# A six-layer decoder on one core: keys leave a PSUM bank by one engine, a second norm takes its variance from the first, and the planner lets layer 1's keys and values fill gaps only

## Chip, core and metric

The kernel runs on one core of a Trainium2 chip. The metric is the device time of one execution in microseconds; each kernel is run several times and the median counts. One more execution was recorded by the hardware profiler. All times below are in microseconds unless marked ns.

The core has five engines that matter here: PE (TensorE, matmuls and transposes into PSUM; PEld is its weight load), DVE (VectorE), ACT (ScalarE), POOL (GpSimd) and SP (SyncE, which issues all DMAs of this kernel). PSUM is used as eight banks of 128 partitions x 512 floats.

## What is computed

A decoder of two post-norm layers on x of shape (8, 256, 256), that is eight sequences (b = 0 to 7) of 256 tokens with 256 features. Each sub-layer is added to its input and normed:

```python
x = ln(x + gated_linear_recurrence(x))                      # l0a
x = ln(x + xattn(x, ctx, ctx, mask, bias))                  # l0x: 16 heads of 16
x = ln(x + ffn0(x))                                         # l0f, below
x = ln(x + self_attn(x, rel_k, rel_v))                      # l1a: relative positions, clipped at 20
x = ln(x + xattn(x, ctx, ctx, mask1))                       # l1x
x = ln(x + swiglu(x))                                       # l1f: hidden 768
# ffn0: a norm of its own, then a quantisation with ONE scale for the whole batch
xn = (x - mu) * rsqrt(var + 1e-5) * gamma + beta
scale = max(abs(xn)) / 127;  xq = round(clip(xn / scale)) * scale
out = xq @ ternary(weight).T
```

`ln` subtracts the mean and divides by sqrt(var + 1e-5), without gain or bias. The one scale of ffn0 is a barrier: no sequence can enter l0f before the last one has left l0x.

## The kernel before, in words

**Tiling.** Per sequence, x is held with tokens on partitions (two tiles of 128 tokens) and, transposed by PE, as xT with features on partitions (two chunks of 128). An attention item (class Item) is one attention of one sequence; ai is 0 for layer 0's cross-attention, 1 for layer 1's self-attention, 2 for layer 1's cross-attention. It has 16 heads, worked in four quads (n = 0 to 3) of four heads.

**One item.** project_q and project_k (line 784) multiply xT or ctxT with weights (PROJ, eight matmuls, one bank) and copy the result out of the bank. Keys are written twice, each time multiplied by par, a column of ones and zeros per partition, so that the heads of even and odd number do not mix (m = 0, 1). For self-attention there are two kinds of keys (k and kr: two different constants are added for far positions). Each piece of keys (chunk c, parity m) was an own step for which the planner picked DVE (line 800) or ACT (line 804). quad (line 845) then issues the scores (line 859) into four banks, at most one quad of an item after another; per head, DVE adds a bias, mask or band and takes the row minimum (line 890, tile sn), ACT takes the exponential (line 906, tile p), PE transposes it (line 470, tile pt), ACT or DVE copies that to SBUF (tile pts, lines 261 and 262), and values (line 929) multiplies it with v (line 944, tile pv). attend_out (line 964) divides by the sums, projects (pso), adds (line 1010) and norms.

**Norms.** norm (line 495) takes bn_stats and bn_aggr on DVE (lines 503, 505), 1/sqrt(var + eps) on POOL as an add and a power (lines 508, 509) and scales on DVE (line 514). own_norm (line 1027) norms l0x once more (tiles st_f0n, rs_f0n, xn), transposes it (ps_xn), applies gamma and beta (xnT, line 1038) and takes the largest absolute value (line 1054, events "amax"). barrier (line 1112) waits for all eight, reduces them over partitions (ps_amax line 1125, gmax, ps_gmax line 1136) and makes the scale; quantised (line 1153) then runs ffn0 per sequence (xq line 1169, psf, yf line 1178, norm l0f, ps_l0f).

**Self-attention's bands.** to_scratch (line 1242) multiplies q with the relative keys (psr line 1252), widens the result on POOL (w, ends; lines 1263, 1266) and writes it to DRAM (sk, line 1272), per chunk c. to_bands (line 1282) fills a band tile on POOL (line 1290) and reads it back skewed, with four DMAs (line 1302), per quad; it sets the event ("band", n). In item_s1 (line 1231) the order was: project_q, to_scratch(0) and to_bands(0), project_k, to_scratch(1) and to_bands(1), a slot of acc, then the first quad. In quad, the scores were issued first and only DVE's step waited for the band.

**Layer 1's cross-attention.** keys_values (line 1468) computes its keys and values from the context alone, once per sequence (psk of ctxT, copied by lines 1479 or 1482; psv of ctxT, copied by line 1503), and stores them in DRAM; it starts once the last item of layer 0 has its q. item_x1 (line 1512) loads them (kin line 1521, vin line 1523), and multiplies the keys with par on DVE (line 1540) or POOL (line 1541).

**The order of work.** Nothing is ordered by loops. Every step is a generator's request to Order.run (line 128): engine, planned cost in us, time at which its inputs are ready. The planner keeps a clock for each engine, and always emits the request with the earliest planned start, in steps of 0.1; ties go by urgency (a smaller number is more urgent: items by 100 + 40 x position, keys_values by 5000 + b). A step that may run on either of two engines takes the one that ends first. Emission fixes each engine's program order, and each engine works through its list in that order. Buffers are slots: p 3, pts 8, q 3, k 2, ctx 2, PSUM banks 8, acc 2; a request for slots waits until they are dropped, the most urgent first. Costs are planned, so a wrong cost changes the order but not what a step takes.

Of the kernel before, what the change touches and what calls it, by code (L numbers as in the profile page):

```python
# [8 lines left out]
F32 = mybir.dt.float32  # L9
# [65 lines left out]

class Order:
# [51 lines left out]
    def run(self):  # L128
        while self.tasks:
            self.serve()  # L130
            best = None
            for task in self.tasks:
# [3 lines left out]
                for engine, cost, emit in ways:  # L136
                    start = max(self.free[engine], ready)
                    if engine == "PE" and kind != self.kind:
                        start += self.TURN[self.kind + kind]
                    late = 0.0 if len(ways) == 1 else start + cost  # L140
                    key = (round(start * 10), task[0], late, task[1])
                    if best is None or key < best[0]:
                        best = (key, task, engine, cost, emit, start, kind)
# [49 lines left out]
def kernel(  # L193
# [80 lines left out]
    half = const.tile([P, NQ], F32, name="half")  # L274
# [220 lines left out]
    def norm(y, t_y, make, name):  # L495

        st = small.tile([P, NQ, 6], F32, tag="ln_st", name=f"st_{name}")
        mv = small.tile([P, NQ, 2], F32, tag="ln_mv", name=f"mv_{name}")
        rstd = small.tile([P, NQ], F32, tag="ln_rs", name=f"rs_{name}")
# [7 lines left out]
        def root():  # L507
            nc.gpsimd.tensor_scalar(rstd, mv[:, :, 1], 1.0, EPS, ALU.mult, ALU.add)
            nc.gpsimd.tensor_tensor(rstd, rstd, half, ALU.pow)

        def scaled():
            dst = make()
            for t in range(NQ):
                nc.vector.tensor_scalar(
                    dst[:, t, :], y[:, t, :], mv[:, t, 0:1], rstd[:, t : t + 1], ALU.subtract,
# [4 lines left out]
        t = yield from do("POOL", 0.95, [t], root)  # L520
        return (yield from do("DVE", 0.68, [t], scaled))
# [98 lines left out]
    def recurrence(b):  # L620
# [9 lines left out]
        def emit():  # L630
# [9 lines left out]
            "POOL", 0.7, [t, a.at],  # L640
# [77 lines left out]
    NS = 2 * KC  # L718

# [35 lines left out]
    def project_q(it, srcT, t_src):  # L755
# [16 lines left out]
        def dve():  # L772
# [6 lines left out]
            [t, t_b, it.q.at], ("ACT", 2 * on_act(256), act), ("DVE", 2 * on_dve(256), dve)  # L779
# [4 lines left out]
    def project_k(it, srcT, t_src, kinds):  # L784
# [9 lines left out]
        it.k, it.t_k = [], []  # L794
        for bufs, bias, biasp, lo, hi in kinds:
            k = yield from get(bufs, f"k{it.name}_{len(it.k)}", t_ps)
            it.k.append(k)
            for c in range(KC):
                for m in range(2):
                    dve = lambda: nc.vector.tensor_scalar(  # L800
                        k.tile[:, c, m, :], ps.tile[:, c, lo:hi], bias(c), par[:, m : m + 1], ALU.add,
                        ALU.mult,
                    )
                    act = lambda: nc.scalar.activation(  # L804
                        k.tile[:, c, m, :], ps.tile[:, c, lo:hi], AF.Identity, bias=biasp(c, m),
                        scale=par[:, m : m + 1],
                    )
                    t = yield from either(
                        [t_ps, t_b, k.at],
                        ("DVE", on_dve(hi - lo) + 0.12, dve), ("ACT", on_act(hi - lo) + 0.09, act),  # L810
                    )
                    it.t_k.append(t)
# [32 lines left out]
    def quad(it, n, parts, bias):  # L845


        c, i = divmod(n, 2)
        if n == 0 and it.ai != 1:
            it.sums = small.tile([P, NQ, H], F32, tag="sums", name=f"sums{it.name}")  # L850
        at = max([it.t_q, *it.t_k])
# [27 lines left out]
        t_bias = 0.0  # L879
        if it.ai == 1:  # L880
            t_bias = yield from event(it.key("band", n))
# [82 lines left out]
    def attend_out(it, t_pv):  # L964
# [47 lines left out]
        ps.drop(t)  # L1012
        t = yield from settle(xb.tile, t, b, it.result, xb.drop)
        events["xs " + it.result, b] = t
        if ai == 0:
            yield from own_norm(b, t)
        elif ai == 1:
# [9 lines left out]
    def own_norm(b, t):  # L1027

        xn = yield from get(y_bufs, f"xn{b}", t)
        t = yield from norm(xs[b], max(t, xn.at), lambda: xn.tile, f"f0n{b}")  # L1030
# [19 lines left out]
        t = yield from either([t], ("DVE", 2 * on_dve(256), dve), ("ACT", 2 * on_act(256), act))  # L1050
# [180 lines left out]
    def item_s1(b, kr_bufs, wide_bufs, acc_bufs, tail_bufs, at_bufs, band_bufs):  # L1231
# [10 lines left out]
        def to_scratch(c, t_sk):  # L1242
# [4 lines left out]
            for t in range(NQ):  # L1247
# [20 lines left out]
                t_w = yield from do("POOL", 0.85, [t_w], emit)  # L1268
# [13 lines left out]
        def to_bands(c, times, sk_set):  # L1282
            for i in range(2):
# [11 lines left out]
                t_f = yield from do("POOL", 0.75, [band.at, it.t_ends[c]], emit)  # L1295
# [26 lines left out]
        def tails_task(n, p, left, t_p):  # L1322
# [33 lines left out]
            t = yield from do("POOL", 1.3, [t_p, tail.at], emit)  # L1356
# [85 lines left out]
        times = yield from to_scratch(1, t_rel)  # L1442
        order.spawn(urgency(it, 0, -19), to_bands(1, times, sk_set))
# [6 lines left out]
        )  # L1450
        events["fed", 1, b] = it.t_q
# [16 lines left out]
    def keys_values(b):  # L1468
# [8 lines left out]
        t_k = []  # L1477
        for c in range(KC):
            dve = lambda: nc.vector.tensor_scalar(
                k.tile[:, c, :], ps.tile[:, c, :], qkb[:, 5, c : c + 1], None, ALU.add  # L1480
            )
            act = lambda: nc.scalar.activation(
                k.tile[:, c, :], ps.tile[:, c, :], AF.Identity, bias=qkb[:, 5, c : c + 1], scale=1.0
            )
            t_k.append(
                (
                    yield from either(
                        [t, t_b, k.at], ("DVE", on_dve(256) + 0.12, dve), ("ACT", on_act(256) + 0.09, act)
                    )
                )  # L1490
            )
        ps.drop(max(t_k))
        t_k = yield from dma(t_k, 262144, lambda: nc.sync.dma_start(out=xk[b], in_=k.tile))
# [18 lines left out]
    def item_x1(b):  # L1512
# [23 lines left out]
        for m in range(2):  # L1536
            dst = k.tile[:, :, m, :]
            t = yield from either(
                [t_k, k.at],
# [252 lines left out]
```

## Time and profile before

| | us |
|---|---|
| three runs | 856.34, 852.46, 856.68 |
| median | 856.34 |
| the profiled execution | 851.82 |
| its span, first to last instruction | 850.1 |
| PE busy | 801.4 (94%) |
| DVE busy | 711.8 (84%) |
| ACT busy | 638.3 (75%) |
| POOL busy | 238.2 (28%) |

How the profile is read: the busy time of an engine is the time in which it has an instruction; matmuls are pipelined, so PE is drawn busy until the modelled end of one. In a timeline a line gives start, length, engine, source line, operation, output tile and inputs, how many instructions are merged (x8), and in brackets how long the engine was idle before and what ended that. In a table by stretches the columns are the busy time of each engine with its instruction count, and then the clock granted to PE (1.00 is full speed). The chain of waits is followed back from the last instruction. Names of tiles leave buffer numbers out: psk<-ctxT,wqk is a projection of keys from the context, psk<-xT_l0f one of layer 1's self-attention.

### The profile page before, as it was taken

How to read it: one execution, taken by the hardware profiler on the slowest of the kernel's cores; microseconds unless marked ns; L12 is line 12 of the kernel's file. 1: busy time of each engine (PE TensorE's matmuls, PEld its weight loads, DVE VectorE, ACT ScalarE, POOL GpSimd, SP SyncE). 2: the span in 40 equal slices, each digit the busy share in tenths (PEclk: the TensorE clock that was granted, in tenths of full speed). 3: DMA queues.
4: the chain of work that ended last, by engine and by line, in shares of the span. 5: the costliest groups of instructions: out<-in, count | busy, mean ns of one | idle time of the engine just before them, and what ended most of it. 6: DMA issues, size and time to landing. Idle time of an engine off the chain costs nothing.

```text
span 850.1 us, 21190 instructions
## 1 busy us (share of the span) xinstructions
PE 801.4 (94%) x7175; PEld 616.7 (73%) x7175; DVE 711.8 (84%) x2495; ACT 638.3 (75%) x2047; POOL 238.2 (28%) x419
## 2 busy tenths in 40 slices
PE   7998999999999988899899999999999998999985
PEld 6785766877777766567667777776777766888885
DVE  3979989998897797788779889898798987889785
ACT  2338987999996445798889898998899895948631
POOL 3440301221121043236144242342152334110020
PEclk9999999999999997999999999999999998999998
DMA  5729511101102446789755546656283432100000
GB/s 174 249 76 105 50 38 39 38 5 35 39 15 75 162 101 150 150 159 194 156 114 111 110 102 134 119 109 141 67 172 67 93 87 76 38 20 7 26 27 25
DMA packets 177681, 77.67 MB, mean 91 GB/s; under 512 B 155046, under 2 KB 171430, under 8 KB 177574
## 3 DMA queue, kind: packets, MB, share of 16 engines
q1 hardware_dynamic: 177574, 76.32, 40.6%
q8 instruction: 57, 0.93, 0.5%
q14 instruction: 50, 0.41, 0.2%
HBM read 41.66 MB, written 34.64 MB: 90 GB/s over the span
## 4 chain that ended last, share of the span: by engine, by line
PE 57%; ACT 15%; DVE 15%; issue 6%; DMA 3%; POOL 3%; SPq 2%; POOLq 0%; DVEq 0%; ACTq 0%
PE pt L470 13%; ACT p L906 9%; PE s L859 8%; PE pv L944 7%; PE psv L487 5%; DVE sn L890 4%; PE psk L476 4%; PE pso L487 4%; PE psq L476 3%; ACT pts L262 3%; PE psd L1667 2%; PE psr L1252 1%; DVE k L800 1%; ACT k L804 1%; SPq L389 1%
## 5 line engine op out<-in xcount | busy, mean ns | idle before, releaser
L906 ACT ACTIVATE p<-sn,nm 128x256 f32<-128x256 f32 x768 | 381.0, 506 | 27.9 <-DVE nm L890 25.6
L470 PE MATMUL pt<-ident,p 128*128 128x128 f32 x1536 | 213.6, 279 | 8.7 <-ACT p L906 2.8
L470 PEld LDWEIGHTS pt<-ident,p 128*128 128x128 f32 x1536 | 172.9, 142 | 52.4 <-ACT p L906 25.1
L262 ACT COPY pts<-pt 128x512 f32<-128x512 f32 x277 | 149.2, 586 | 39.3 <-PE pt L470 34.4
L906 ACT ACTIVATION_READ_ACCUMULATOR p<-sn,nm 128x1 f32 x768 | 151.6, 197 | 0.0
L859 PE MATMUL s<-k,q 32*128 32x256 f32 (+2 forms) x1792 | 134.0, 375 | 3.2 <-DVE nm L890 2.4
L859 PEld LDWEIGHTS s<-k,q 32*128 32x128 f32 x1792 | 87.5, 186 | 34.4 <-issue 14.0
L890 DVE CUSTOM_DVE_ANT_0 sn<-s,hide 128x256 f32<-128x256 f32 x256 | 93.7, 417 | 15.4 <-PE s L859 8.7
L944 PE MATMUL pv<-pts,v 128*32 128x256 f32 x1536 | 104.8, 384 | 0.7 <-ACT pts L262 0.7
L890 DVE CUSTOM_DVE_ANT_0 sn<-s,band 128x256 f32<-128x256 f32 x256 | 93.6, 416 | 12.9 <-ACT p L906 7.7
L890 DVE CUSTOM_DVE_ANT_0 sn<-s,bias 128x256 f32<-128x256 f32 x256 | 94.4, 419 | 10.1 <-ACT p L906 7.5
L261 DVE COPY pts<-pt 128x512 f32<-128x512 f32 x107 | 71.7, 683 | 4.3 <-PE pt L470 3.6
L944 PEld LDWEIGHTS pv<-pts,v 128*32 128x32 f32 x1536 | 43.1, 109 | 41.3 <-issue 17.9
L890 DVE DVE_READ_ACCUMULATOR2_ANT nm<- 128x1 f32 x768 | 62.9, 82 | 0.0
L975 POOL COPY rsw<-rsum 128x512 f32<-128x512 f32 x24 | 14.7, 612 | 130.3 <-DVE rsum L969 122.8
L487 PE MATMUL pso<-wvo,oT 128*128 128x256 f32 x192 | 47.9, 394 | 0.2 <-DVE oT L990 0.2
L487 PEld LDWEIGHTS pso<-wvo,oT 128*128 128x128 f32 x192 | 36.2, 196 | 6.7 <-DVE oT L990 1.4
L1290 POOL COPY band<-ends 64x256 f32<-64x256 f32 x64 | 22.3, 372 | 44.8 <-DVE nm L890 44.8
L1263 POOL COPY w<-w 128x504 f32<-128x504 f32 x32 | 19.6, 613 | 53.3 <-DVE w L261 31.4
L1362 DVE TENSOR_REDUCE acc<-tail 128x8 f32<-128x864 f32 x32 | 33.3, 1042 | 0.6 <-POOL tail L1351 0.6
L487 PE MATMUL psv<-wvo,ctxT 128*128 128x256 f32 x128 | 31.0, 385 | 0.1
L476 PE MATMUL psk<-ctxT,wqk 128*128 128x256 f32 x128 | 30.9, 384 | 0.0
(201 smaller groups left out, 1364.8 us busy)
## 6 DMA issues: line engine op xcount, KB each, us to landing
sk<-w SPq DMA_DIRECT2D x32, 416.0 KB
band<-sk SPq DMA_DIRECT2D x64, 104.0 KB
pb<-p SPq DMA_DIRECT2D x64, 104.0 KB
band<-sk SPq DMA_DIRECT2D x64, 84.0 KB
pb<-p SPq DMA_DIRECT2D x64, 84.0 KB
acc<-pb SPq DMA_DIRECT2D x32, 156.0 KB
ctxT<-in_ctxT SPq DMA_DIRECT2D x16, 256.0 KB
wpad<-in_qk_w SPq DMA_DIRECT2D x6, 512.0 KB
```

What stands on the lines that cost most here:

```text
L261: ("DVE", on_dve(n), lambda: nc.vector.tensor_copy(dst, src)),
L262: ("ACT", on_act(n), lambda: nc.scalar.copy(dst, src)),
L470: nc.tensor.transpose(ps[:, c, t * P : (t + 1) * P], src[:, t, c * P : (c + 1) * P], ident)
L476: nc.tensor.matmul(ps, w[:, c, lo:hi], rhs[:, c, :], start=(c == 0), stop=(c == KC - 1))
L487: nc.tensor.matmul(ps[:, t, :], srcT[:, c, t * P : (t + 1) * P], w[:, c, :], start=(c == 0), stop=(c == KC - 1),)
L859: nc.tensor.matmul(ps[j].tile[:, t, first : first + w], it.q.tile[32 * j : 32 * j + 32, c, t * P : (t + 1) * P], k[32 * j : 32 * j + 32, c ...
L890: nc.vector.tensor_tensor_reduce(out=s.tile[:, t, :], in0=ps[j].tile[:, t, :], in1=tile[:, t, :], scale=-1.0, scalar=3e38, op0=ALU.add, op ...
L906: nc.scalar.activation(p.tile[:, j, q, :], s.tile[:, q, :], AF.Exp, bias=nm[:, q : q + 1], scale=-1.0, accum_out=it.sum_of(q, h),)
L944: nc.tensor.matmul(it.pv.tile[32 * j : 32 * j + 32, c, :], it.v.tile[:, k, head_of(n, j), :], pts.tile[:, k, :], start=(k == 0 and i == 0 ...
L1263: nc.gpsimd.tensor_copy(w.tile[:, :, NR:], w.tile[:, :, NR - 1 : NR].to_broadcast([P, HH, PBW - NR]))
L1290: nc.gpsimd.tensor_copy(band.tile[0:BLK, :, t, lo:hi], it.ends[c][0:BLK, t, i:HH:2].unsqueeze(2).to_broadcast([BLK, 4, hi - lo]),)
L1362: lambda: nc.vector.tensor_reduce(acc[:, c, :, own, 1], tail.tile, AX.X, ALU.add),
```

## The change

- **The planner** (Order.run): a step of keys_values (urgency at or above FILLER, 5000) is looked at last, and is passed over on an engine if some other task could start there before the step's own start plus 0.6 of its cost. Nothing else about keys_values' place changes.
- **Keys** (project_k, keys_values): all pieces of one kind of keys are now one step on one engine. On DVE it is two instructions that write both parities at once (scalar_tensor_tensor with par broadcast); on ACT the same four as before.
- **Norm**: for l0x, norm makes both outputs from one set of statistics. With v the variance of the first norm, the second's factor is (v (1 + eps) + eps^2)^(-1/2), an added POOL instruction and a power over twice as many columns. The tile xn is scaled first, then x. own_norm's statistics and root go.
- **Scores**: in quad a self-attention's scores are planned no earlier than 2 us (AHEAD) before the planned time of their band, after the event ("band", n). In item_s1 the first quad is spawned after to_scratch(0) and project_k; to_scratch(1) and to_bands(1) come after it, and after the slot of acc.
- **item_x1**: keys times par on DVE only.
- **Planned costs**: norm's root 0.95 to 0.9 (1.1 with two factors), scaling 0.68 to 0.66, POOL's a and first widening step 0.7 to 0.57 and 0.85 to 0.7, a band's fill 0.75 to 0.64, the tails 1.3 to 1.06, q and xnT on DVE 0.68 to 0.79, the first gate matmuls 1.0 to 0.95.

```diff
+FILLER = 5000
 class Order:
     def run(self):
-            best = None
-            for task in self.tasks:
+            best, soon = None, {}
+            for task in sorted(self.tasks, key=lambda t: t[0] >= FILLER):
...
+                    if task[0] < FILLER:
+                        soon[engine] = min(soon.get(engine, start), start)
+                    elif soon.get(engine, 1e9) < start + 0.6 * cost:
+                        continue
...
-    def norm(y, t_y, make, name):
+    def norm(y, t_y, make, name, make2=None):
...
         def root():
-            nc.gpsimd.tensor_scalar(rstd, mv[:, :, 1], 1.0, EPS, ALU.mult, ALU.add)
-            nc.gpsimd.tensor_tensor(rstd, rstd, half, ALU.pow)
+            nc.gpsimd.tensor_scalar(rstd[:, 0], mv[:, :, 1], 1.0, EPS, ALU.mult, ALU.add)
+            if n == 2:
+                nc.gpsimd.tensor_scalar(
+                    rstd[:, 1], mv[:, :, 1], 1.0 + EPS, EPS * EPS, ALU.mult, ALU.add
+                )
+            nc.gpsimd.tensor_tensor(rstd[:, 0:n], rstd[:, 0:n], half[:, 0:n], ALU.pow)
...
+        if n == 2:
+            t_2 = yield from do("DVE", 0.66, [t_r], lambda: scaled(make2, 1))
+        t = yield from do("DVE", 0.66, [t_r], lambda: scaled(make, 0))
...
     def project_k(it, srcT, t_src, kinds):
-            for c in range(KC):
-                for m in range(2):
-                    dve = lambda: nc.vector.tensor_scalar(
-                        k.tile[:, c, m, :], ps.tile[:, c, lo:hi], bias(c), par[:, m : m + 1], ALU.add,
-                        ALU.mult,
-                    )
...
+            def dve():
+                for c in range(KC):
+                    nc.vector.scalar_tensor_tensor(
+                        k.tile[:, c], ps.tile[:, c, lo:hi].unsqueeze(1).to_broadcast([P, 2, n]), bias(c),
+                        par.unsqueeze(2).to_broadcast([P, 2, n]), ALU.add, ALU.mult,
+                    )
...
+            t_e = max(t_e, (yield from either(
+                [t_ps, t_b, t_e, k.at], ("DVE", KC * on_dve(2 * n), dve), ("ACT", 4 * on_act(n) + 0.36, act)
+            )))
...
     def quad(it, n, parts, bias):
+        t_bias = 0.0
+        if it.ai == 1:
+            t_bias = yield from event(it.key("band", n))
...
-        at = max([it.t_q, *it.t_k])
+        at = max([it.t_q, *it.t_k, t_bias - AHEAD])
...
-        t_bias = 0.0
-        if it.ai == 1:
-            t_bias = yield from event(it.key("band", n))
...
     def attend_out(it, t_pv):
+        if ai == 0:
+            xn = yield from get(y_bufs, f"xn{b}", t)
+            t, t_n = yield from norm(
+                xb.tile, max(t, xn.at), next_x(b, it.result), f"{it.result}{b}", lambda: xn.tile
+            )
+            xb.drop(t)
+            yield from own_norm(b, xn, t_n)
+            return
...
     def item_s1(...):
-        times = yield from to_scratch(1, t_rel)
-        order.spawn(urgency(it, 0, -19), to_bands(1, times, sk_set))
         it.acc = yield from get(acc_bufs, f"acc{it.name}")
...
             quad(it, 0, parts, lambda n, j: (it.bands[n].tile[:, j], 0.0)),
         )
+        times = yield from to_scratch(1, t_rel)
+        order.spawn(urgency(it, 0, -19), to_bands(1, times, sk_set))
...
     def item_x1(b):
-            t = yield from either(
-                [t_k, k.at],
-                ("DVE", 0.33, lambda: nc.vector.tensor_scalar(dst, kin.tile, par[:, m : m + 1], None, ALU.mult)),
-                ("POOL", 0.62, lambda: nc.gpsimd.tensor_scalar(dst, kin.tile, par[:, m : m + 1], None, ALU.mult)),
+            t = yield from do(
+                "DVE", 0.35, [t_k, k.at],
+                lambda: nc.vector.tensor_scalar(
+                    k.tile[:, :, m, :], kin.tile, par[:, m : m + 1], None, ALU.mult
+                ),
             )
```

In keys_values the two pieces of the stored keys become one step of two instructions on one engine, in the same way.

## The prediction

> **What bounds it now.** I read the page first, then the busy time by stretches, then the chain of waits where a stretch was thin.
>
> The page, then the stretches (from:to, length, then busy time and instructions of PE, PEld, DVE, ACT and POOL, then granted clock, DMA share, GB/s):
>
> ```profile
> span 850.1 us, 21190 instructions
> PE 801.4 (94%) x7175; PEld 616.7 (73%) x7175; DVE 711.8 (84%) x2495; ACT 638.3 (75%) x2047; POOL 238.2 (28%) x419
> ```
> ```profile
> 60.00:263.00 203.00, 198.35 (x1798) 148.19 (x1798) 182.82 (x734) 179.71 (x618) 36.56 (x54) 1.00 0.26 38
> 263.00:292.00 29.00, 28.90 (x170) 23.52 (x169) 18.87 (x53) 13.66 (x27) 4.50 (x8) 1.00 0.40 137
> 292.00:350.00 58.00, 48.87 (x326) 36.98 (x327) 48.02 (x149) 29.51 (x79) 19.38 (x47) 0.88 0.58 138
> 350.00:700.00 350.00, 338.09 (x3513) 246.45 (x3513) 302.92 (x1141) 314.90 (x1058) 125.88 (x230) 1.00 0.58 122
> 700.00:725.00 25.00, 21.47 (x180) 16.38 (x182) 19.11 (x64) 14.98 (x50) 10.42 (x11) 0.86 0.21 65
> ```
>
> TensorE is the bound nearly everywhere: 198.35 of 203 us, 338.09 of 350. No edit takes a matmul away, so a gain can only be time in which PE stands idle or runs at a lower clock. The thin stretch is 292 to 350, the passage from layer 0 to layer 1: 58 - 48.87 = 9.1 us idle, and in two windows of 6.8 us the clock is 0.5:
>
> ```profile
> 317.80:324.60 6.80, 5.43 (x17) 4.04 (x17) 5.34 (x13) 1.61 (x3) 2.31 (x6) 0.50 0.92 247
> 331.40:338.20 6.80, 6.67 (x41) 5.56 (x42) 6.42 (x30) 5.12 (x18) 2.56 (x7) 0.50 0.42 105
> ```
>
> At half clock 6.8 us do the work of 3.4, so these cost 2 x 3.4 = 6.8 us more: 15.9 us lost here in all. The next place is 700 to 725: 3.5 us idle and one half-clock window, 3.4 us: 6.9.
>
> 263 to 292 looks full, but with what? The chain of waits from 262 to 304 begins:
>
> ```profile
> by line: PE psv L487 29.3%; PE psk L476 28.8%; PE pt L470 6.6%; issue 5.8%; PE pv L944 5.3%; PE psq L476 4.7%; PE psf L487 4.6%; PE pso L487 4.1%; PE ps_xn L470 2.9%; ACT xk L1482 2.3%; ACT xq L1169 1.5%; PE ps_rs L470 1.4%; ACT xT_l0f L262
> ```
>
> These psk and psv are the keys and values of layer 1's cross-attention (keys_values), which nothing needs before the first kin load at 388.5. 58% of the chain that leads to the barrier is work that could wait.
>
> **Fillers (FILLER in Order.run).** The change lets a keys_values step onto an engine only if no other task could start there before 0.6 of its planned cost: 1.04 us for a projection of 1.73. What were the steps that stood behind them? The last exp of the last layer-0 item ends at 266.98, its last pv at 274.50. Without fillers: transposes 0.44, copy 0.58, pv 1.00, about 269.3, so 5.2 us sooner. (The pts copies at 271.68 waited for a pv that stood behind two projections.) Later pso stood 0.2 us behind a psk (oT multiplied at 276.43, pso at 276.65), amax's transpose 1.3 us (288.30 to 289.62), the spread of gmax 1.0 (290.50 to 291.55), the first xq 0.6 behind an xk copy (293.60 to 294.31 with its hand-over). Sum 5.2 + 0.2 + 1.3 + 1.0 + 0.6 = 8.3 us. Against it: a filler may still start 0.4 x 1.73 = 0.7 us too early at each of about five PE steps, up to 3.5. Kept: 4.8 to 8.3.
>
> **Own norm.** Removed eight times: stats 0.75, aggregate 0.30, two POOL steps 0.19 and 0.70; only the last item's are on the path to the barrier (the others, 8.4 us of DVE in all, lie under the 98% PE of 60 to 263). Before: root of l0x at 280.44, xn finished at 285.72, 5.3 us. After: one more POOL step (0.19, 0.08 gap), the power on four columns instead of two (no row; between 0.70, the row for two, and twice that; I take 0.70, its nearest row), then xn at once, 0.73: 2.0 to 2.7 us. Gain 2.6 to 3.3. x itself is scaled 0.73 later; its reader yf (295.73) is covered.
>
> Barrier sooner by 7.4 to 11.6 us. But the projections go somewhere: 16 x 1.73 = 27.7 us of PE, and 12 of the 16 run before 291.7 now. Those displaced land behind the barrier, in the stretch that has 15.9 us to give. So 15.9 is also the ceiling.
>
> **Keys leave by one engine.** ACT and DVE took pieces in turn, and the timeline shows that they do not overlap:
>
> ```profile
> 312.73 0.56 ACT L804 ACTIVATE k<-psk,bklp,par 128x256 f32<-128x256 f32 x1
> 313.33 0.54 DVE L800 TENSOR_SCALAR k<-psk,bkl,par 128x256 f32<-128x256 f32 x1
> 313.91 0.56 ACT L804 ACTIVATE k<-psk,bklp,par 128x256 f32<-128x256 f32 x1 [0.61 <-DVE k L800]
> 314.51 0.54 DVE L800 TENSOR_SCALAR k<-psk,bkl,par 128x256 f32<-128x256 f32 x1 [0.64 <-ACT k L804]
> ```
>
> 0.59 us a piece, 3.9 us for a self-attention item's eight (312.73 to 316.58). On ACT alone, by the q pair (0.84 for two, 0.42 each): 4 x 0.42 + 4 x 0.33 = 3.0. On DVE the change uses two instructions of 512 outputs; nearest row sg<-sg,fu 0.68 (yf 0.73): 1.4 for the first kind, 0.7 for the narrow one, 2.1. A broadcast par has no row: 0.9 (two plain pieces' 0.45 each) to 1.65 (two of x_l1a's 0.825) for one instruction bound it, I take 0.68. So 0.9 to 1.8 us per item, on the path only for the first two items (their k is in the chain at 312 to 328): within the 15.9. For the rest PE works through: at nothing, and a microsecond each way if not. The xk pair of a filler (0.47 on ACT, 0.48 on DVE) goes the same way, 0.1 us, off the path.
>
> **Scores earlier, and held.** quad is now spawned before the second to_scratch. The first scores ran at 327.87, though their keys were out at 316.58 and PE stood idle from 314.5 to 317.65. What moves behind: two psr (0.56), two copies, POOL 0.60 + 0.19 twice, two sk DMAs, then eight band DMAs (SP: six took 4.12, so 5.5 us) for quads 2 and 3. Cover: quads 0 and 1, eight heads of some 1.0 us ACT. acc is now taken ahead of it, free unless item b-2 is unfinished: 0 to a few us, I take 0. The added condition (scores no earlier than 2 us before the planned band) adds no wait on the chip; it orders PE's queue. Cost 0 to one quad's scores, 1.12 us, per quad; taken at 0, since of 256 band steps only two waited for a DMA (2.0 us). If that cover is gone, see rival D.
>
> **x1 keys on DVE.** Fourteen POOL steps of 1592 ns (22.2 us, planned at 0.62) go. DVE gets them; its two in the trace took 0.62 and 0.83, nearest else xnT 0.45: +6 to +12 us of DVE in a stretch where it is 303 of 350 busy. On the path at one place:
>
> ```profile
> 706.07 3.10 POOL L1541 TENSOR_SCALAR k<-kin,par 128x512 f32<-128x512 f32 x2
> 709.12 0.87 POOL L1554 COPY v<-vin 128x512 f32<-128x512 f32 x1
> 710.08 0.19 POOL L508 TENSOR_SCALAR rs_l1a<-mv_l1a 128x2 f32<-128x2 f32 x1
> ```
>
> The statistics were ready at 709.21, but POOL was still at the steps queued behind the keys: 0.9 us. x_l1a then took 2.80 for two, beside POOL's cast and add, and PE idled 3.12. Gain 1, at most the 6.9 of that stretch. The other planner costs (0.57, 1.06, 0.64, 0.79) only reorder: 0, plus or minus 5, from the 12 us that PE idles in 350 to 700 (half of it either way).
>
> Against this: x_l1a averages 825 ns for a step that xn does in 409, and POOL works beside x_l1a. The Trainium skill, SBUF — State Buffer, "Who interferes with whom", names a cause: VectorE's fast SBUF-to-SBUF modes and GpSimd lock one port pair for a whole instruction, and the later one blocks. The rows agree so far; rival E prices it.
>
> **Sum.** Barrier stretch: 7.4 to 11.6 from the two terms, ceiling 15.9, taken 10 (63%); 700 to 725: 1; the rest 0. 851.8 (the profiled execution; span 850.1 and 1.7 around it) - 11 = 841. The runs' median is 856.3, 4.5 above; I add about 3 of that: **844**. Own range 836 to 851.
>
> On the clock, the Trainium skill (TensorE: Matmul & The Clock Gate, "HAM oscillation") warns of idle gaps above some 3.4 us. Here PE gaps of 3.2 us (ps_l0f at 317.65, waiting for DVE's x_l0f) and 1.7 us (the same at 331.53) stand ahead of the half-clock windows, which speaks against so high a threshold; by the rule alone neither gap would throttle, the ceiling would be 9.1 and the forecast 851.8 - 0.63 x 9.1 - 1 + 3 = 848, inside the same range.
>
> **Rivals.**
> B, everything is recovered: 851.8 - 15.9 - 6.9 = 829, plus 3: 832 (829 to 836). For it: fillers are just the cover those gaps lack. Against: VectorE is 48 of 58 us busy there, and most idle time waits for its norms. Chance 0.13.
> C, given back: layer 1 is PE-bound, the displaced projections meet it, their results hold PSUM banks and pts slots while waiting for a gap on DVE (84% busy), and two of them can hold both ctx slots that kin and vin need. If the last projection runs after 388.5, the first cross-attention item starts late, and the 10 us return through 350 to 700: 844 + 10 = 854, within 852 to 860. Chance 0.12.
> E, DVE behind POOL: each of fourteen key steps waits up to one xb add (1.28 us), 18 us; with half of them ahead of a head's scores on the path, 9 back: 851.8 - 11 + 9 + 3 = 853. Against: DVE has 350 - 303 = 47 us idle in 350 to 700, and 22.2 us of POOL are gone. Chance 0.05.
> D, slower: scores that were ready in PSUM when a band landed now run after it. Price 1.12 us of scores for each of 32 quads, 36 at most; on top of the forecast it passes 860.6 from (860.6 - 844) / 1.12 = 15 exposed quads; at 22 it is 844 + 25 = 869. Against: bands were late twice. Chance 0.16.
>
> **Numbers.** The forecast has 0.54. Half a per cent, about what a measurement of this kernel can tell from no change, is 852.1 to 860.6: faster is the forecast and B, 0.67; same is C and E, 0.17; slower is D, 0.16. Range 829 to 860 leaves out D.
>
> **What would show it.** Right: psk and psv of ctxT leave the chain ahead of ps_gmax, which comes 7 us or more before 291.5; no st_f0n; k pieces back to back; first scores before 320; fewer half-clock windows in 290 to 350. Wrong: DVE sn waiting for s after a band (D); psv of ctxT after 388 (C); k<-kin on DVE far above 0.72 (E); new half-clock windows after 350.

## The result, and the profile after

| | before | after |
|---|---|---|
| median of four runs, us | 856.18 (852.46 to 856.68) | 846.37 (844.07 to 848.76) |
| ratio | 1 | 0.9895, 95% interval 0.9853 to 0.9937 |
| the profiled execution, us | 851.82 | 848.76 |
| its span | 850.1 | 847.0 |

The change is about 1.05% faster by the ratio, which is estimated over all runs, and 9.8 us by medians; 844 was predicted. One warning before any trace is read: the profiled execution of before was the fastest of its four runs and that of after the slowest, so this pair of traces differs by 3.1 us only. What the traces can tell is where each stage gained or lost, not the sum.

The page of after:

```profile
span 847.0 us, 21156 instructions
PE 792.0 (94%) x7175; PEld 606.7 (72%) x7175; DVE 705.2 (83%) x2445; ACT 634.0 (75%) x2042; POOL 208.9 (25%) x396
```

The number of matmuls is the same, as it must be; POOL has lost 29 us and DVE, which was to get the keys of layer 1's cross-attention, has not grown. Busy time by stretches (columns as before):

```profile
60.00:263.00 203.00, 193.46 (x1768) 145.41 (x1766) 174.18 (x684) 175.00 (x601) 32.99 (x46) 0.99 0.26 40
...
292.00:350.00 58.00, 53.24 (x379) 39.65 (x379) 50.75 (x166) 39.54 (x102) 21.16 (x51) 0.97 0.72 141
350.00:700.00 350.00, 334.38 (x3455) 240.72 (x3451) 300.96 (x1114) 299.35 (x1016) 103.33 (x213) 1.00 0.64 123
700.00:725.00 25.00, 23.31 (x232) 17.63 (x225) 22.66 (x79) 19.49 (x67) 8.98 (x10) 1.00 0.31 96
```

Read the second row against that of before. In 292 to 350, the stretch in which nearly everything was to be won, PE does 379 matmuls instead of 326, is busy 53.24 us instead of 48.87, and its clock is 0.97 instead of 0.88. Now the third row: 334.38 busy instead of 338.09, 3455 matmuls instead of 3513. Something that was won in the passage is given back in layer 1. (In the first row PE is busy 5 us less too; e1 below, the same program, idles 4 us less there, so that is a matter of this execution.)

The barrier itself did not come sooner. PE's timeline in after, from ps_amax to ps_gmax:

```profile
292.29 0.27 PE L1155 MATMUL ps_amax<-ident,amax 128*1 128x128 f32 x1 [2.12 <-DVE amax L1150]
292.42 3.32 PE L483 MATMUL psk<-ctxT,wqk 128*128 128x256 f32 x8
295.67 0.58 PE L1166 MATMUL ps_gmax<-gmax,ones 1*128 1x1 f32 x2
```

In before it stood here:

```profile
291.55 0.38 PE L1136 MATMUL ps_gmax<-gmax,ones 1*128 1x1 f32 x2
```

Now it is 4.1 us later, of which 1.8 were there at layer 0's last pv already (it ended at 276.25, before at 274.50). The middle line of after is a filler (a step of keys_values), exactly what the rule was to keep out of this place, and most of it ran at half clock (granted 0.5 from 292.9 to 296.3; 3.32 us for what takes 1.89 elsewhere).

### The profile page after: what moved, and what is told of

Its sections match the earlier page's. It is cut to its first block, busy times and chain, and to the rows that moved or that the text cites. A ratio compares the mean times of both kernels' runs of the same rounds, so it can differ in the third digit from the quotient of the medians.

```text
span 847.0 us, 21156 instructions
## 1 busy us (share of the span) xinstructions
PE 792.0 (94%) x7175; PEld 606.7 (72%) x7175; DVE 705.2 (83%) x2445; ACT 634.0 (75%) x2042; POOL 208.9 (25%) x396
## 5 line engine op out<-in xcount | busy, mean ns | idle before, releaser
L477 PE MATMUL pt<-ident,p 128*128 128x128 f32 x1536 | 209.0, 277 | 9.8 <-ACT p L932 4.6
L477 PEld LDWEIGHTS pt<-ident,p 128*128 128x128 f32 x1536 | 170.4, 141 | 52.3 <-ACT p L932 27.2
L269 ACT COPY pts<-pt 128x512 f32<-128x512 f32 x273 | 145.8, 589 | 28.0 <-PE pt L477 25.2
L932 ACT ACTIVATION_READ_ACCUMULATOR p<-sn,nm 128x1 f32 x768 | 153.7, 200 | 0.0
L888 PE MATMUL s<-k,q 32*128 32x256 f32 (+2 forms) x1792 | 128.2, 374 | 2.9 <-DVE nm L916 1.6
L888 PEld LDWEIGHTS s<-k,q 32*128 32x128 f32 x1792 | 84.1, 186 | 32.3 <-issue 18.9
L268 DVE COPY pts<-pt 128x512 f32<-128x512 f32 x111 | 74.4, 684 | 8.4 <-PE pt L477 6.3
L494 PE MATMUL pso<-wvo,oT 128*128 128x256 f32 x192 | 46.1, 383 | 2.4 <-DVE oT L1016 2.4
L1293 POOL COPY w<-w 128x504 f32<-128x504 f32 x32 | 19.5, 609 | 74.0 <-ACT w L269 42.6
L1667 ACT ACTIVATE sg<-fg 128x512 f32<-128x512 f32 x24 | 13.9, 594 | 24.6 <-PE fg L1656 16.8
```

What stands on the lines that cost most here:

```text
L268: ("DVE", on_dve(n), lambda: nc.vector.tensor_copy(dst, src)),
L269: ("ACT", on_act(n), lambda: nc.scalar.copy(dst, src)),
L477: nc.tensor.transpose(ps[:, c, t * P : (t + 1) * P], src[:, t, c * P : (c + 1) * P], ident)
L494: nc.tensor.matmul(ps[:, t, :], srcT[:, c, t * P : (t + 1) * P], w[:, c, :], start=(c == 0), stop=(c == KC - 1),)
L888: nc.tensor.matmul(ps[j].tile[:, t, first : first + w], it.q.tile[32 * j : 32 * j + 32, c, t * P : (t + 1) * P], k[32 * j : 32 * j + 32, c ...
L932: nc.scalar.activation(p.tile[:, j, q, :], s.tile[:, q, :], AF.Exp, bias=nm[:, q : q + 1], scale=-1.0, accum_out=it.sum_of(q, h),)
```

## The experiments

### One theory and its rivals

Two kinds of explanation stood against each other. One takes the total as a sum of the parts: leave one out, and the total loses what that part was worth. The other, the theory of the re-deal (D in the expectations), says that every edit deals the planner's order anew, as cards are dealt: a step is emitted by its planned start in tenths, so a small shift changes which of two tasks goes first, and hundreds of later choices with it; then leave-one-out totals show the deal and not the part, and only what recurs over several deals belongs to a part. Within it there are two stage theories: that the fillers' rule fills the passage from layer 0 to layer 1, and that the scores' spawn (the first quad ahead of the second to_scratch) and hold (scores planned no earlier than 2 us before their band) change layer 1. Twelve kernels were run. The median of before was 855.7, 851.4 and 857.3 in the three sets of runs (e1 to e4, e5 to e8, e9 to e12), so ratios to it are compared, not times.

**e1, after again.**

> The changed kernel once more, for a second profile: its one profile (848.8) is the slowest of its four runs, and that of the kernel before (851.8) the fastest of its four, so the pair shows 3 us of a difference of 9.8. All theories: 844 to 849. In the profile, the theory that the passage between the layers carries the gain expects ps_gmax again at 295 +- 1.5 us (4 later than before), the first scores at 328 +- 2, and a lead over the kernel before of 5 to 8 us at about 355.

Measured 846.12 against 855.71: 0.9896 (0.9868 to 0.9924). The result holds, and ps_gmax (293.66) and the first scores (326.23) came where they were expected. Its runs go from 844.34 to 850.99 for one and the same program, so a single profiled time is worth some 0.4% either way.

**e2, without the rule for fillers.**

```diff
-                    elif soon.get(engine, 1e9) < start + 0.6 * cost:
-                        continue
```

> The changed kernel without the rule that passes a filler over; all else stays. Theory P (the passage between the layers carries the gain, and the fillers' rule is its larger part): 851 to 856. Theory R (the rule sees only requests already posted, so it keeps no chain step free, ps_gmax even came 4 us later; the gain is the early scores, the keys and the cross-attention's keys): 844 to 849, ps_gmax no later than 295. Theory D (every edit only re-deals the list): anywhere from 840 to 856.

Measured 853.65: 0.9976 (0.9959 to 0.9994). Its stretch from 292 to 350:

```profile
292.00:350.00 58.00, 46.85 (x325) 34.20 (x325) 48.51 (x156) 37.00 (x89) 20.25 (x50) 0.88 0.63 119
```

That is inside what the theory of the passage had expected, and ps_gmax came at 298.65, later than the rival R allowed. The row is nearly that of before: 325 matmuls, clock 0.88. All else of the change is in this kernel; take the rule out, and the passage is as thin as it was. Its last ctxT projection stands at 298.3, that of after at 316.8. So in this deal the rule's worth is the cover it saves up for the time behind the barrier.

**e3, the own norm with its own statistics and root again**, the rest of after kept.

```diff
+        t = yield from settle(xb.tile, t, b, it.result, xb.drop)
+        events["xs " + it.result, b] = t
         if ai == 0:
             xn = yield from get(y_bufs, f"xn{b}", t)
-            t, t_n = yield from norm(
-                xb.tile, max(t, xn.at), next_x(b, it.result), f"{it.result}{b}", lambda: xn.tile
-            )
-            xb.drop(t)
+            t_n = yield from norm(xs[b], max(t, xn.at), lambda: xn.tile, f"f0n{b}")
             yield from own_norm(b, xn, t_n)
...
```

> The changed kernel, but the feed-forward's norm takes statistics and a root of its own again (xn made from l0x). P: the barrier later by 2.6 to 3.3 us, 849 to 850, ps_gmax at 298 to 299. R: the passage is bound by DVE and PE behind the barrier, so at most 1 us, 846 to 848. D: 840 to 856.

Measured 862.95: 1.0083 (1.0065 to 1.0102), 16.8 us more than e1, for leaving out a part that makes one norm 2.9 us shorter, and outside every range that had been expected, that of the re-deal too. A sum of parts cannot give this. The trace says where the 16.8 are: from the statistics to xn it takes 5.3 us (2.4 in after), yet layer 1 is entered at 337.8, 1.3 us *before* after does; from there to the end it takes 523 us, in after 508. The loss lies in a stage that the edit does not touch.

**e4, scores spawned and issued as before.** The call of quad goes behind the second to_scratch again, and the wait for the band's event back to DVE's step.

```diff
-        at = max([it.t_q, *it.t_k, t_bias - AHEAD])
+        at = max([it.t_q, *it.t_k])
...
+        times = yield from to_scratch(1, t_rel)
+        order.spawn(urgency(it, 0, -19), to_bands(1, times, sk_set))
         it.acc = yield from get(acc_bufs, f"acc{it.name}")
```

> The changed kernel with the scores as before: the first quad spawned after the second to_scratch, scores planned without regard to the band. P: the passage loses its cover, half-clock windows come back in 300 to 350, 851 to 854. R: the same sign, 849 to 854, since the early scores are most of what is left. The forecast's slower rival (scores held behind bands cost time): faster than 846, below 844. D: 840 to 856.

Measured 845.83: 0.9882 (0.9858 to 0.9905), the same as after. Both stage theories had expected 849 or more. In this deal the part had no net effect.

**e5 and e6, a planned cost of no meaning changed by 0.01 us**, in after and in before:

```diff
-        do("DVE", 0.7, [t_s, t_b, t_bias, s.at], emit)
+        do("DVE", 0.71, [t_s, t_b, t_bias, s.at], emit)
```

> A control: the changed kernel with one planned cost moved by a hundredth, the band-or-mask step of a head on DVE from 0.70 to 0.71 us. What the chip is asked to do is the same; only the list is dealt anew. Theory D (any edit moves the time by the re-deal alone): 5 us or more away from 846.2, either way. If the stages' mechanisms rule: 843 to 849.

> The same control on the kernel before: that cost from 0.70 to 0.71. D: 5 us or more away from 855.7, either way. Mechanisms rule: 853 to 858.

Measured 857.62 and 859.91 against 851.38: 1.0067 (1.0044 to 1.0089) and 1.0096 (1.0074 to 1.0119). The work is the same; only its order differs, and here and there which of two engines a step went to. Yet after is 1.7% slower than itself, before 1.0%, as the theory of the re-deal had expected. The 0.01 us moves the time as much as the whole change does. This settles how e3 must be read.

**e7, early spawn without the hold; e8, the hold without the early spawn.** e7 takes the first part of e4's diff alone (no hold; the wait for the band's event goes back to DVE's step), e8 its second part (no early spawn).

> The changed kernel without the hold: the first quad is still spawned ahead of the second to_scratch, but scores are planned without regard to their band. In the profile with both, the passage gained 8 us over the one with neither, and 350 to 500 gave them back. If the hold gives them back: 836 to 842, and the lead over the kernel before at about 355 (6 to 8 us) is kept to 480. If the early scores themselves only borrow the time: 844 to 850. D: no order, 840 to 856.

> The changed kernel with the hold, but the first quad spawned after the second to_scratch as before. If the hold gives time back: 848 to 854, since the early scores that paid for it are gone. If the early scores only borrow: 844 to 847. D: no order, 840 to 856.

Measured 833.98: 0.9799 (0.9774 to 0.9823), and 838.13: 0.9852 (0.9816 to 0.9887). e7 is the fastest kernel of the study; its ratio, applied to the 855.7 of the first set, is 838.5, in the range expected if the hold gives time back. e8, 843.0 in the same way, was expected at 844 to 854 by both theories of the stage and fits neither.

**e9 to e12: third deals.** The planned cost of e5 at 0.69 in before (e9), in after (e10) and in e7's kernel (e12), and at 0.71 in e7's kernel (e11).

> A third deal of the kernel before: the same planned cost at 0.69 us. So far its deals stand at 1.000 and 1.010 of it. Re-deal alone: 0.985 to 1.015. Stage theory, for this and the next three: whatever the total, kernels without the fillers' rule enter layer 1 (first pv behind ps_gmax) at 339 us or later and lose 14 us or more of PE in the passage; those with it enter at 339 or earlier and lose 11 or less.

> A third deal of the changed kernel, the cost at 0.69. Its deals stand at 0.990 and 1.007. Re-deal alone: 0.985 to 1.015. If the change is worth something over deals, the mean of its three lies 0.005 or more below that of the kernel before's three. Stage theory: enters layer 1 at 339 or earlier, passage losses 11 or less.

> The kernel with early scores and no hold, a second deal (0.71); its first stands at 0.980. If leaving out the hold is a gain of its own: 0.975 to 0.988. If 0.980 was a lucky deal: 0.990 to 1.010. Stage theory: enters layer 1 at 339 or earlier.

> The kernel with early scores and no hold, a third deal (0.69). As the second deal: 0.975 to 0.988 if the hold costs time by itself, 0.990 to 1.010 if its first deal was lucky.

Measured against 857.25: e9 843.95, 0.9842 (0.9801 to 0.9883); e10 841.41, 0.9825 (0.9779 to 0.9870); e11 844.94, 0.9853 (0.9800 to 0.9907); e12 841.64, 0.9829 (0.9772 to 0.9885). e9 and e10 lie just below the 0.985 to which the re-deal was expected to reach; e11 and e12 are in the range expected if the hold costs time by itself. Before with a lucky cost is no slower than after with the cost that it came with. The passage in e9 and in e10, the same cost, without the change and with it:

```profile
292.00:350.00 58.00, 46.24 (x321) 34.55 (x322) 46.84 (x155) 33.81 (x91) 21.22 (x50) 0.88 0.68 127
```
```profile
292.00:350.00 58.00, 55.20 (x446) 40.62 (x443) 52.13 (x179) 41.33 (x125) 25.53 (x60) 1.00 0.82 161
```

125 matmuls more in 58 us, and no half-clock window: e10 leaves the passage 13 us ahead (first pv of layer 1 at 328.5, in e9 at 341.6) and still ends only 3.6 us ahead (spans 838.7 and 842.3).

### What recurs over the deals

Worked out from the timelines of all fourteen profiles: "passage" is from layer 0's last pv to layer 1's first, "lost" there is PE's idle time and half of the half-clock windows; then PE's busy time from 350 to 490, and the start of the first k<-kin, the keys of layer 1's first cross-attention. The last column is the time from the start of PE's 2700th matmul (at 353 to 374) to that of its 4000th. Each profile has 7175 matmuls, so their number marks how far the kernel has come, if roughly, since the kinds come in another order.

| kernel | sn cost | rule | spawn, hold | ratio | first pv of layer 1 | lost in the passage | PE 350 to 490 | first k<-kin | 2700th to 4000th matmul |
|---|---|---|---|---|---|---|---|---|---|
| before | 0.70 | no | neither | 1 | 339.8 | 14.9 | 134.8 | 396 | 130.6 |
| e6 | 0.71 | no | neither | 1.0096 | 347.1 | 25.5 | 130.6 | 408 | 137.9 |
| e9 | 0.69 | no | neither | 0.9842 | 341.6 | 19.2 | 132.0 | 400 | 138.0 |
| e2 | 0.70 | no | both | 0.9976 | 343.1 | 18.0 | 129.7 | 431 | 146.6 |
| after | 0.70 | yes | both | 0.9895 | 339.1 | 8.9 | 129.7 | 428 | 143.0 |
| e1 | 0.70 | yes | both | 0.9896 | 337.0 | 8.6 | 129.4 | 430 | 145.2 |
| e5 | 0.71 | yes | both | 1.0067 | 333.9 | 8.3 | 132.6 | 421 | 145.6 |
| e10 | 0.69 | yes | both | 0.9825 | 328.5 | 3.7 | 129.0 | 422 | 150.7 |
| e3 | 0.70 | yes | both | 1.0083 | 337.8 | 3.9 | 131.9 | 429 | 147.4 |
| e4 | 0.70 | yes | neither | 0.9882 | 335.8 | 10.3 | 134.9 | 401 | 132.1 |
| e8 | 0.70 | yes | hold only | 0.9852 | 331.5 | 7.5 | 133.2 | 404 | 136.0 |
| e7 | 0.70 | yes | early only | 0.9799 | 329.8 | 10.2 | 136.3 | 400 | 132.7 |
| e11 | 0.71 | yes | early only | 0.9853 | 335.5 | 9.3 | 132.0 | 409 | 133.9 |
| e12 | 0.69 | yes | early only | 0.9829 | 329.6 | 3.5 | 134.8 | 402 | 133.4 |

Three columns sort the kernels by a part without one exception, whatever the deal.

*Lost in the passage* goes by the rule: 14.9 to 25.5 us in the four kernels without it, 3.5 to 10.3 in the ten with it; on average 19.4 and 7.4. (Ahead of e9 and e10, 14 or more and 11 or less had been expected.) Layer 1 is entered 9 us sooner on average (342.9 and 333.9). Three of the four lack all other parts of the change as well; e2 alone takes away the rule and nothing else, in one deal, and with 18.0 it lies with the three.

*First k<-kin* goes by spawn and hold together: 421 to 431 in the six kernels with both, 396 to 409 in the other eight. The line in after, in e10, and in e7:

```profile
428.28 1.40 DVE L1570 TENSOR_SCALAR k<-kin,par 128x512 f32<-128x512 f32 x2
```
```profile
421.56 1.29 DVE L1570 TENSOR_SCALAR k<-kin,par 128x512 f32<-128x512 f32 x2 [0.39 <-PE s L888]
```
```profile
399.73 1.88 DVE L1570 TENSOR_SCALAR k<-kin,par 128x512 f32<-128x512 f32 x2
```

Nothing is wrong with these instructions; it is their place that tells. They wait for a slot of keys (in e10 the bracket names the scores that end the wait). The load before them (kin) was issued at 404.6 in after and at 389.5 in e7, and from it to k<-kin it takes 22.8 to 26.5 us in the six kernels, 5.3 to 17.3 in the eight. In after and e10, four self-attention items write their keys before the first cross-attention does (the fourth at 385.9 and 383.9); in e7, and in before, the order is three, the cross-attention, the fourth (419.1 in e7). There are two slots of keys, and the fourth item holds one. That the fourth comes first is not the whole of it: in e8, with the hold alone, it does too (395.4), but there the third item's scores run through, the slot comes free, and k<-kin follows at 403.6. In all six kernels with both, 14 quads of self-attention's scores run ahead of k<-kin, so the fourth item has begun its scores, too; in the others 10 to 12. So from 410 to 440 DVE adds bands in after, which in e7 it hardly does (time and instructions of DVE on tile band are the first pair after the length; after, then e7):

```profile
410.00:440.00 30.00, 13.98 (x38) 0.00 (x0) 2.01 (x6) 1.00 0.81 144
```
```profile
410.00:440.00 30.00, 0.74 (x2) 0.00 (x0) 2.00 (x6) 1.00 0.61 131
```

and the whole stretch behind the passage, 350 to 490, is thinner (after, e10, e7, e12):

```profile
350.00:490.00 140.00, 129.66 (x1286) 91.29 (x1278) 111.55 (x396) 104.04 (x352) 44.29 (x98) 0.99 0.81 144
```
```profile
350.00:490.00 140.00, 129.02 (x1198) 90.60 (x1202) 105.18 (x371) 101.14 (x333) 41.91 (x89) 0.96 0.85 145
```
```profile
350.00:490.00 140.00, 136.25 (x1394) 100.33 (x1396) 118.97 (x433) 121.28 (x407) 43.31 (x95) 0.99 0.67 132
```
```profile
350.00:490.00 140.00, 134.78 (x1395) 100.45 (x1390) 117.60 (x439) 122.64 (x410) 43.63 (x93) 0.99 0.69 132
```

PE is busy 130.4 us on average over the six, 133.6 over the eight, and ACT, which makes the exponentials, 101 to 104 against 121 to 123 in these four rows. The DMA engines are fuller (0.81 and 0.85 against 0.67 and 0.69): bands go through DRAM, and four self-attention items in a row have all of theirs here. PE's busy time does not sort as cleanly as the place of the keys does (e6, without either edit, has 130.6).

*2700th to 4000th matmul* does: 143.0 to 150.7 us in the six, 130.6 to 138.0 in the eight, on average 146.4 and 134.3. So spawn and hold together cost some 12 us in this stage. That the late keys and the bunching of the bands are why is my reading of these rows and not shown by a run of its own.

What it costs in the total, by deals of equal cost, after against early-only: 0.9895 and 0.9799, 1.0067 and 0.9853, 0.9825 and 0.9829. So 1.0%, 2.1% and nothing. Against e4 and e8, of the cost 0.70, it is 0.1% and 0.4%. With the rule in all of them, the five kernels with both go from 0.9825 to 1.0083 (0.9953 on average) and the five without both from 0.9799 to 0.9882 (0.9843); only e10 lies among the others. So some 1% over the deals, with a scatter as large.

## Why the prediction was right or wrong

The time was 2.4 us from the forecast and the sign was right. The steps behind it were not all right, and that the number came out so well is luck. By the 2700th matmul after led before by 4.7 us (362.3 and 367.1). The next 1300 took 12.4 us longer than in before (143.0 and 130.6), for a stage that I had put at nothing, and the rest 10.8 us less (334.4 and 345.2), of which I had forecast 1. The pair of traces ends 3.1 us apart.

**What bounds the kernel; the ceiling.** Held for the passage: time was to be had there, and PE's lost 14.9 us there (15.9 in my window) fell to 8.9. Its gain in after, 6.0, is smaller than the 10 I took; in the deals of 0.71 and 0.69 it is 17.2 and 15.5.

**Fillers: "barrier sooner" by 4.8 to 8.3. This step failed in its mechanism.** ps_gmax came at 295.67, and not 7.4 to 11.6 us before 291.55, as this term and the norm's gave. I read the rule as one that keeps fillers behind the chain. But it compares a filler with requests that have been *posted*, and a chain step on PE is posted only when its predecessor on DVE or POOL has been emitted. While the chain is on another engine, PE's list of posted steps is empty, and a filler goes out. (This is read from the code; no run changes it.) Seven fillers still stand between layer 0's last pv and ps_gmax (eight before), and from the end of that pv to ps_gmax it takes 19.4 us (17.1 before); over the ten kernels with the rule, 15.4 to 19.5. I also took 58% of the chain that leads to the barrier for fillers, in a window that ran to 304; up to ps_gmax it is 71%. DVE's timeline of after shows one doing harm on another engine as well:

```profile
282.12 0.69 DVE L1036 TENSOR_TENSOR xb<-pso,xb 128x512 f32<-128x512 f32 x1 [1.10 <-PE pso L494]
283.78 0.88 DVE L1510 TENSOR_SCALAR xk<-psk,qkb 128x256 f32<-128x256 f32 x2 [0.97 <-PE psk L483]
284.57 0.74 DVE L513 BATCH_NORM_STATS2 st_l0x<-xb 128x6 f32<-128x256 f32 x2
285.24 0.30 DVE L515 BATCH_NORM_AGGREGATE mv_l0x<-st_l0x 128x2 f32<-128x6 f32 x2
287.20 0.74 DVE L528 TENSOR_SCALAR xn<-xb,mv_l0x,rs_l0x 128x256 f32<-128x256 f32 x2 [1.67 <-POOL rs_l0x L523]
```

xb was out at 282.81, but its statistics began at 284.57: the copy of a filler was ahead in DVE's list, and DVE stood 0.97 us idle until that filler's projection had ended. 1.7 us of the barrier's chain went there. The rule gained all the same, by what I had called the projections that "go somewhere": it holds some of them back until behind the barrier, where they fill the gaps of ffn0. Of the 16, 5 to 7 run after ps_gmax in the ten kernels with the rule, 0 to 4 in the four without (5 in after, 4 in before). ps_gmax moved by +4.1 us, -5.2 and -5.2 in the deals of 0.70, 0.71 and 0.69, but so did layer 0's last pv ahead of it, by +1.8, -7.2 and -3.5; the time lost in the passage moved by -6.0, -17.2 and -15.5.

**Own norm: 5.3 to between 2.0 and 2.7.** Right: the lines above give 285.54 to 287.94, 2.4 us, in every kernel with the edit. POOL's part of it:

```profile
285.62 0.19 POOL L518 TENSOR_SCALAR rs_l0x<-mv_l0x 128x2 f32<-128x2 f32 x1 [9.38 <-DVE mv_l0x L515]
285.88 0.19 POOL L520 TENSOR_SCALAR rs_l0x<-mv_l0x 128x2 f32<-128x2 f32 x1
286.15 1.02 POOL L523 TENSOR_TENSOR rs_l0x<-rs_l0x,half 128x4 f32<-128x4 f32 x1
```

The power on four columns takes 1.02 us, not the 0.70 that I took, inside the bounds of 0.70 to 1.40. Whether the 3 us count in the total is not shown: e3 does not tell, since its passage loses no more than that of after. While PE has a filler to do, a shorter norm should gain little, but that is argued, not shown.

**Keys by one engine.** The groups of after, by form:

```profile
L1570 DVE TENSOR_SCALAR k<-kin,par 128x512 f32<-128x512 f32 x16 | 9.9, 631 | 0.0
L822 DVE SCALAR_TENSOR_TENSOR k<-psk,bkl,par 128x512 f32<-128x512 f32 x14 | 9.8, 745 | 1.8 <-PE psk L483 1.8
L528 DVE TENSOR_SCALAR x_l1a<-xb,mv_l1a,rs_l1a 128x256 f32<-128x256 f32 x16 | 9.7, 644 | 1.1 <-POOL rs_l1a L523 1.0
...
L822 DVE SCALAR_TENSOR_TENSOR k<-psk,bkl,par 128x216 f32<-128x216 f32 x12 | 4.6, 425 | 0.0
```

0.745 us for 512 outputs with two broadcast operands (0.68 taken, bounds 0.9 to 1.65 for one that reads a broadcast: it is below both), 0.425 for the narrow one; an item's keys on DVE alone take 2.2 us by the timeline's merged lines (1.40 and 0.78), on ACT 3.4 (1.93 and 1.44), before 3.9. Sized well; no kernel took this part alone away, so its share of the total is open.

**Scores earlier, and held: "Cost 0". This is the term that was mis-sized.** The first scores started at 328.25, not before 320, because the keys themselves were late (ACT began the first at 320.75 after 1.74 us of waiting for its projection). In e10, e7 and e12 they start at 317 to 318, so the forecast of the step holds in some deals. Where scores meet a late band (rival D), the price is small: from 350 to 490 DVE's band steps waited for scores for 3.4 us in after, 1.3 in before. It was elsewhere: spawn and hold together let the third and the fourth self-attention go by turns, and the first cross-attention's keys came some 24 us later (427 on average against 402, no overlap), in a stage that takes some 12 us longer. I had written that the condition "orders PE's queue" and then asked only what that does to PE's next steps, not which item takes the key slots.

**x1 keys on DVE.** The price is right: 0.631 us instead of 1.592 on POOL. The gain of 1 us is not shown. 700 to 725 has 23.31 us busy at clock 1.00 in after instead of 21.47 at 0.86. But in e6 and e9, where POOL still multiplies the keys, it is as full and at the same clock:

```profile
700.00:725.00 25.00, 24.97 (x274) 18.31 (x273) 21.07 (x80) 21.75 (x77) 6.21 (x7) 1.00 0.30 79
```
```profile
700.00:725.00 25.00, 22.97 (x236) 17.47 (x228) 23.38 (x87) 23.17 (x81) 9.62 (x11) 1.00 0.30 96
```

Nor is it the edit that brought x_l1a from 825 to 644 ns: in e6 and e9 it averages 589 and 625. The times of single instructions say more. In after, 7 of the 16 x_l1a ran with POOL idle, in 400 to 412 ns, and 9 beside a POOL instruction, in 472 to 1533; of the 16 k<-kin, 10 took 471 to 483 and the 6 beside POOL 475 to 1391. The Trainium skill, SBUF — State Buffer, "Who interferes with whom", says that a VectorE instruction in a two-port mode and GpSimd lock one port pair, and that the later of the two waits for the whole of the other's instruction. The trace agrees, as all long ones are beside POOL; no run here isolates it. So rival E (DVE behind POOL) is right as a mechanism, and its size is not: the six cost some 2.5 us in all, where I had put 18.

**Re-deal: "0, plus or minus 5". Far too narrow.** 0.01 us in a planned cost moved after by +1.7% and -0.7%, before by +1.0% and -1.6%: 6 to 15 us. My range of 829 to 860 held the result, but of the deals measured e7, with one part less, is at 834 and e5 at 858, so the range was not too wide.

**The rivals.** B (all recovered, 832): not in after; e10's passage does lose only 3.7 us. C (given back in layer 1): its condition did not come true, the last ctxT projection ran at 316.8 and not after 388.5, but its outcome did in part, by the late keys: by equal cost the 2700th matmul comes 4.7, 17.5 and 9.7 us sooner than in before's kernel, the 4000th 7.7 later, 9.9 sooner and 3.1 later, and the span ends 3.1, 3.9 and 3.6 sooner. D: not seen as a mechanism, the place was right. On the clock: half-clock windows in the passage cost 6.8 to 10.2 us without the rule and 0 to 3.4 with it.

**What stays open.** How much of the 1.05% the change owns. By equal costs after stands to before as 0.9895 to 1, 1.0067 to 1.0096, 0.9825 to 0.9842; only the first pair's intervals are apart. The mean over three deals is 0.9929 for after, 0.9979 for before, 0.9827 for the early spawn without the hold; the first two are 0.005 apart, just what I had asked for beforehand as a sign of a gain. Three deals with such a scatter don't prove a half per cent; that all three have the same sign speaks for a gain, if weakly. Which of the planner's choices makes the third and the fourth self-attention go by turns was not traced. And e7's is the version to take, but part of its 2.0% is its deal: its two other deals gave 0.9853 and 0.9829.

## What to carry to other kernels

Where a planner with planned costs orders the work, run the unchanged kernel and the changed one with a meaningless 0.01 us on a cost before you believe any total: here that was worth as much as the change. Judge a part by a stage's measure that sorts all deals (PE time lost in the passage, place of the first cross-attention's keys, time for a given number of matmuls), not by the total when it is left out. A rule that lets filler work wait must know the chain's next step before it is posted, and one that holds a task back must be asked what else now takes its slots.

## What the runs showed of the hardware

- A power on POOL took 0.70 us for 128x2 and 1.02 for 128x4; a straight line through these two rows would be 0.16 a column above 0.38 (an estimate).
- One instruction for 512 outputs from PSUM with two broadcast operands took 0.745 us on DVE; two plain ones of 256 took 0.54 each by the timeline of before.
- The same multiplication of 128x512 by a column took 1.592 us on POOL and 0.631 on DVE, where it was 0.471 to 0.483 with POOL idle.
- A scaling of 128x256 on DVE (x_l1a) took at most 0.417 us in all fourteen profiles when POOL was idle beside it, and up to 2.085 (in before) when it was not.
- Half-clock windows between 20 and 800 us came in lengths of 3.4, 6.8 and, once (e12, at 337.5), 10.2 us. In after one lies directly behind a PE wait of 4.81 us (105.1), one behind 2.12 us (292.9).
- The same program on the same chip went from 844.34 to 850.99 us in six runs, 0.8%.
